# Two groups of transposes in an attention kernel take their PSUM from another ring of buffers

## The chip, the cores and the metric

The kernel runs on one core of a Trainium2 chip. A core has a matrix engine (TensorE, "PE" in the profile, with its weight loads as "PEld"), a vector engine (VectorE, "DVE"), a scalar engine (ScalarE, "ACT"), GpSimd ("POOL") and a queue that issues transfers ("SP"). Each engine works through its own instructions in order and waits on semaphores for the others. TensorE writes its products into PSUM, which VectorE and ScalarE read. The metric is the device time of one execution in microseconds, as a median of several.

## What is computed

The reference is a stack of two transformer layers over four sequences of 1024 tokens with 256 channels. What matters here are its three kinds of attention, all with 16 heads of 16 channels:

```python
x = x + _L0_attn_ref(_layernorm(x), ...)   # causal, with a bias that grows with the key's position
x = x + _L0_ffn_ref(_layernorm(x), ...)    # 4 experts, top 2 of them per token; each expert is an
                                           # attention among the tokens that chose it
x = x + _L1_attn_ref(_layernorm(x), ...)   # causal, with rotary positions
x = x + _L1_ffn_ref(_layernorm(x), ...)    # 64 experts, top 8, and one shared

# each of the first three holds, per sequence and head:
scores = jnp.einsum('bhtd,bhsd->bhts', q, k) * scale
attn = jax.nn.softmax(jnp.where(mask, scores, -inf), axis=-1)
y = jnp.einsum('bhts,bhsd->bhtd', attn, v)
```

## The kernel before, in words

**Units.** An attention is worked off in units: four heads (one of four groups `g`) of up to 512 queries of one sequence. A sequence of 1024 tokens has two halves of queries, so 8 units; an expert's sequence has as many query tiles of 128 as its fullest batch needs, in one or two halves. In the profiled execution there are 160 units: 32 in the attention of layer 0, then 32, 16, 16 and 32 in the four experts (six, two, three and seven tiles, as the widths of the instructions show), then 32 in the attention of layer 1. `nq` is the number of a unit's query tiles (2 to 4).

**Two passes over the scores.** The scores are computed twice. First with queries on the partitions: two heads of a pair against up to 512 keys (L294, tile `s1`), of which VectorE takes the row maxima (L309; in causal attention it first adds a mask to the diagonal block, L306). These are the *products for maxima*. When a unit has all its maxima, `set_max` reduces and negates them (L365), transposes them on TensorE (L372, tile `pm`, one transpose for each query tile), and VectorE adds the result into a spare row of the queries (L376), so that the second pass has the maximum already subtracted. In the second pass keys are on the partitions: L329 writes one bank for each of two heads (tile `s2`), ScalarE takes the exponential out of each (L340), and L394 multiplies by the values, for all keys of the unit into one bank (`av`). These are the *products for exponentials*. In causal attention L353 adds a mask to the diagonal ones.

**The end of a unit.** `divide` lets ScalarE copy the finished `av` into SBUF (L408, tile `avs`), TensorE transposes it (L412, tile `py`), and VectorE takes the reciprocal of the sums (L416) and multiplies (L417).

**Ticks.** The order of TensorE, VectorE and ScalarE is written out by hand in `_run_attention`. In each tick it emits, for TensorE: one step of maxima of a unit that is ahead (the two heads of one L294 pair), one step of exponentials of a unit that is behind (the two heads of an L329 pair), the masks, and the L394 of the step one to three ticks earlier; for VectorE the reduction of this tick; for ScalarE the exponentials. `next_max` picks the two steps so that they use different strips of the matrix engine, and the profile shows their products overlapping. A unit's exponentials come `lead` ticks after its maxima. Then, at the end of the tick, one to a few of the *running parts* get a step, in rotation: `set_max`, `divide`, the projections of queries, keys and values (L177, L194), the output projection (L436, L445), a layer norm's transposes (L104), the transposes of an expert's rows (L939). A part that something needs at once is run to its end (`settle`). So the transposes of `set_max` and `divide` stand at the end of a tick, ahead of the next tick's L294.

**PSUM.** `open_attention` lays out all of it, counted in banks of 512 floats on each partition:

```python
self.ps = ctx.enter_context(tc.tile_pool(name="ps", bufs=2, space=PSUM))
self.ps_m = ctx.enter_context(tc.tile_pool(name="ps_m", bufs=3, space=PSUM))
self.ps_av = ctx.enter_context(tc.tile_pool(name="ps_av", bufs=1, space=PSUM))
```

`ps` is a ring of two buffers of two banks. The products for maxima take one buffer a tick, and so does each of the running parts that project or transpose (tags "s"). `ps_m` is a ring of three buffers of one bank; the products for exponentials take two a tick (tag "t"), and in the kernel before `pm` and `py` take one each. `ps_av` is one bank. A tile of a ring takes the buffer that was taken longest ago, in the order in which the program asks; its first write waits until the last reader of that buffer's earlier tile is done. At the end of a run of the attention, when no maxima are left, a tick does two steps of exponentials, the second in a buffer of `ps` (tile `s3`, L346).

Of the kernel before, what the change touches and what calls it, by code (L numbers as in the profile page):

```python
# [10 lines left out]
F32 = mybir.dt.float32  # L11
# [10 lines left out]
P = 128  # L22
# [22 lines left out]
class Kernel:  # L45
# [313 lines left out]
    def set_max(self, u):  # L359

        nc = self.nc
        nq = u["nq"]
        self.n_mx += 1
        m = self.mx_buf[self.n_mx % 2]
        nc.vector.tensor_reduce(  # L365
            m[:, 0:nq, :, ROW_MAX], u["mx"][:, 0:nq, :, 0 : u["n_half"]], AX.X, ALU.max, negate=True
        )
        yield
        yield
        pm = self.ps_m.tile([P, 512], F32, tag="t", name="pm")  # L370
        for q in range(nq):
            nc.tensor.transpose(  # L372
                pm[:, q * P : (q + 1) * P], m[:, q].rearrange("p h r -> p (h r)"), self.ident
            )
        part = u["qk"][0][:, u["q0"] : u["q0"] + nq * P]
        nc.vector.tensor_tensor(part, pm[:, 0 : nq * P], part, ALU.add)  # L376
        yield
# [25 lines left out]
    def divide(self, u):  # L403

        nc = self.nc
        g, nq, i0 = u["g"], u["nq"], u["q0"] // P
        avs = self.p2.tile([P, 512], F32, tag="avs", name="avs")
        nc.scalar.copy(avs[:, 0 : nq * P], u["av"][:, 0 : nq * P])  # L408
        yield
        pt = self.ps_m.tile([P, 4, 4, 32], F32, tag="t", name="py")  # L410
        for q in range(nq):
            nc.tensor.transpose(  # L412
                pt[:, q].rearrange("p h r -> p (h r)"), avs[:, q * P : (q + 1) * P], self.ident
            )
        rec = self.p2.tile([P, 4, 4], F32, tag="rec", name="rec")
        nc.vector.reciprocal(rec[:, 0:nq], pt[:, 0:nq, :, HD])  # L416
        nc.vector.tensor_tensor(  # L417
            u["job"]["y"][:, i0 : i0 + nq, 64 * g : 64 * (g + 1)].rearrange(
                "p q (h d) -> p q h d", d=HD
            ),  # L420
            pt[:, 0:nq, :, 0:HD],
            rec[:, 0:nq].unsqueeze(3).to_broadcast([P, nq, 4, HD]),
            ALU.mult,
        )
        yield
# [39 lines left out]
    def _run_attention(self, jobs, causal):  # L465
# [76 lines left out]
        for tick in range(len(ahead) + lead + 4):  # L542
# [40 lines left out]
            for u in full:  # L583
                if divides[1:]:
                    settle(divides[-2])
                begin("divide", u, divide(u), True)
                divides.append(u["divide"])
                if u["g"] == NG - 1 and u["last"]:
                    begin("finish", u, finish(u))
                    ended.append(u["finish"])  # L590
# [1022 lines left out]
```

## Time and profile before

| | |
|---|---|
| median of 7 runs | 4624.06 us (4615.11 to 4635.45) |
| the profiled execution | 4632.74 us |
| its span, first to last instruction | 4631.0 us |
| busy: TensorE, VectorE, ScalarE, GpSimd | 4354.3, 2634.8, 1910.5, 628.4 us |
| granted clock of TensorE, mean | 0.954 |

By stretches of the span (us, busy time of each engine, granted clock):

| stretch | what runs | PE | DVE | ACT | clock |
|---|---|---|---|---|---|
| 0 to 950 | attention of layer 0 | 891.06 | 609.77 | 400.29 | 0.95 |
| 950 to 1745 | expert of six tiles | 765.78 | 444.65 | 384.82 | 0.96 |
| 1745 to 1925 | expert of two tiles | 161.06 | 78.21 | 64.41 | 0.98 |
| 1925 to 2200 | expert of three tiles | 252.87 | 133.33 | 109.14 | 0.97 |
| 2200 to 3150 | expert of seven tiles | 928.67 | 574.28 | 486.31 | 0.97 |
| 3150 to 4300 | attention of layer 1 | 1054.29 | 695.54 | 381.45 | 0.92 |
| 4300 to 4631 | the rest of the experts of layer 1 | 300.56 | 99.03 | 84.11 | 0.97 |

How to read what follows. A row of the timeline has a start and a duration in microseconds, then the engine, the line of the kernel, the operation, what it writes and reads, and the shapes; "x2" means two instructions merged into one row. A bracket tells how long the engine was idle before it and whose release ended that. A group's row ends with the busy time of all its instructions, the mean of one in ns, and the idle time before them with the releasers. "issue" is idle time that no release ended. Matmuls are pipelined, and their ends are modelled, so a busy TensorE isn't one at its peak.

The two groups of the change, from the tiles' views: the 544 instructions of L372 have a median of 273 ns (270 to 476), those of L412 too (272 to 477); L376 comes 160 times (414 to 693 ns), L416 160 times (198 to 259 ns), L417 160 times (291 to 426 ns).

### The profile page before, as it was taken

To read this page: it belongs to the slowest core of one execution; us is meant where nothing else is said; L and a number is where in the kernel's file an instruction comes from. 1 tells how busy PE (TensorE), PEld (TensorE's weight loads), DVE (VectorE), ACT (ScalarE), POOL (GpSimd) and SP (SyncE) were. 2 spreads that over 40 slices of the span, in tenths; PEclk is the share of its full clock that TensorE was granted. 3 is DMA by queue.
4 is the path that set the end of the run, shared out by engine and by line. 5 is a ranking of instruction groups with operands and counts; after the bars stand their busy time and mean duration, and the time that the engine had idled before them with its cause. 6 is when DMAs were issued, how large, how long until landed. Compare 5 with 4: busy or idle time off the path is not lost.

```text
span 4631.0 us, 88434 instructions
## 1 busy us (share of the span) xinstructions
PE 4354.3 (94%) x38042; PEld 2055.4 (44%) x38042; DVE 2634.8 (57%) x4505; ACT 1910.5 (41%) x4087; POOL 628.4 (14%) x671
## 2 busy tenths in 40 slices
PE   7999999979999999898999999997999999998898
PEld 3444445444444445444343434443444444443556
DVE  5766676646556544454666666655767566474232
ACT  1444444525555553343454545451343333233331
POOL 1002020110000000000001010102111423415243
PEclk8999999979999999999999999998999899898999
DMA  6004000010000000000000000001000111102576
GB/s 217 2 2 136 6 20 4 29 39 8 8 8 8 8 30 25 23 26 26 1 9 27 14 27 1 27 10 32 6 1 28 65 37 49 58 29 88 139 183 176
DMA packets 134455, 188.93 MB, mean 41 GB/s; under 512 B 14816, under 2 KB 116448, under 8 KB 133216
## 3 DMA queue, kind: packets, MB, share of 16 engines
q1 hardware_dynamic: 91584, 99.11, 6.8%
q0 software_dynamic: 27264, 66.18, 5.1%
q10 hardware_dynamic: 15136, 17.20, 1.2%
q8 instruction: 314, 5.14, 0.5%
q14 instruction: 157, 1.29, 0.1%
HBM read 83.36 MB, written 99.09 MB: 39 GB/s over the span
## 4 chain that ended last, share of the span: by engine, by line
PE 64%; DVE 6%; issue 5%; DMA 2%; ACT 1%; another core or an unknown queue 1%; POOL 0%; SPq 0%; POOLq 0%; DVEq 0%; ACTq 0%
PE s L294 20%; PE av L394 12%; PE s L329 8%; PE pq L177 3%; PE pa L177 3%; PE pb L177 2%; PE pk L177 2%; DVE mx L309 2%; PE pv L194 2%; PE po L445 2%; PE pgu L1292 2%; PE py L412 1%; PE pm L372 1%; DMA xg<-xs 1%; PE s L353 1%
## 5 line engine op out<-in xcount | busy, mean ns | idle before, releaser
L340 ACT ACTIVATE e<-s 128x512 f32<-128x512 f32 (+3 forms) x3428 | 1546.1, 498 | 1857.2 <-PE s L329 1065.7
L309 DVE TENSOR_REDUCE mx<-s 128x2 f32<-128x1024 f32 (+3 forms) x1760 | 1724.8, 981 | 757.1 <-PE s L329 600.5
L329 PE MATMUL s<-qa,ka 32*128 32x384 f32 (+3 forms) x7040 | 1882.2, 557 | 58.6 <-ACT e L340 31.1
L294 PE MATMUL s<-ka,qa 32*128 32x384 f32 (+3 forms) x7040 | 1709.0, 565 | 69.3 <-DVE mx L309 27.2
L394 PE MATMUL av<-e,v 128*32 128x256 f32 (+3 forms) x14080 | 949.7, 346 | 22.2 <-ACT e L346 11.2
L294 PEld LDWEIGHTS s<-ka,qa 32*128 32x128 f32 x7040 | 551.3, 190 | 673.0 <-issue 406.3
L329 PEld LDWEIGHTS s<-qa,ka 32*128 32x128 f32 x7040 | 721.9, 187 | 139.4 <-ACT e L340 68.7
L394 PEld LDWEIGHTS av<-e,v 128*32 128x32 f32 x14080 | 298.7, 111 | 793.6 <-issue 711.8
L306 DVE TENSOR_TENSOR s<-s,mask 128x256 f32<-128x256 f32 x512 | 218.8, 427 | 244.2 <-PE s L294 184.5
L975 POOL DMA_DIRECT2D xc<-os x24 | 18.1, 756 | 2004.3 <-DVE os L971 2004.3
L1270 POOL DMA_INDIRECT xs<-rowsx,dest x192 | 185.4, 966 | 222.9 <-DVE dest L1269 155.4
L353 PEld LDWEIGHTS <-ident_b 128*32 128x32 bf16 x4096 | 62.6, 96 | 244.6 <-issue 231.0
L353 PE MATMUL s<-mask_kq,ident_b 128*32 128x128 bf16 x4096 | 154.3, 231 | 0.0
L177 PE MATMUL pq<-xT,wq 128*128 128x512 f32 (+2 forms) x384 | 149.6, 528 | 2.0 <-ACT xT L942 1.7
L93 POOL TENSOR_SCALAR rows<-x,rstd,shift 128x256 f32<-128x256 f32 x96 | 52.1, 558 | 720.7 <-DVE shift L82 710.9
L445 PE MATMUL po<-wo,yT 128*128 128x256 f32 x544 | 129.7, 390 | 11.5 <-ACT yT L440 11.5
L177 PE MATMUL pk<-xT,wk 128*128 128x512 f32 (+2 forms) x384 | 139.1, 499 | 0.1
L963 DVE SCALAR_TENSOR_TENSOR ka<-pk,bk,kc 128x768 f32<-128x768 f32 (+3 forms) x64 | 52.3, 818 | 152.5 <-PE pk L177 152.5
L1441 POOL DMA_INDIRECT sum<-ye,idx x64 | 100.0, 1562 | 161.0 <-DVE ye L1439 115.1
L376 DVE TENSOR_TENSOR qa<-pm,qa 128x512 f32<-128x512 f32 (+2 forms) x160 | 97.1, 607 | 40.7 <-PE pm L372 37.5
L958 ACT ACTIVATE qa<-pq,bq 128x768 f32<-128x768 f32 (+3 forms) x64 | 47.4, 741 | 173.8 <-PE pq L177 173.8
L445 PEld LDWEIGHTS po<-wo,yT 128*128 128x128 f32 x544 | 101.1, 192 | 36.9 <-ACT yT L440 17.2
(205 smaller groups left out, 3271.3 us busy)
## 6 DMA issues: line engine op xcount, KB each, us to landing
xc<-empty SPq DMA_DIRECT2D x4, 4096.0 KB
gu<-in_e_gu SPq DMA_DIRECT2D x64, 256.0 KB
xs<-empty ACTq DMA_DIRECT2D x16, 642.0 KB
xg<-xs SPq DMA_DIRECT2D x64, 160.5 KB
dn<-in_e_dn SPq DMA_DIRECT2D x64, 128.0 KB
sum<-sum SPq DMA_DIRECT2D x12, 512.0 KB
rows<-xc SPq DMA_DIRECT2D x19, 256.0 KB
xc<-os POOLq DMA_DIRECT2D x8, 512.0 KB
```

Source lines behind the costliest of these rows:

```text
L177: nc.tensor.matmul(pt[:, h, 0:wd], lhsT=w[:, c, g * P : (g + 1) * P], rhs=xnT[:, c, h * 512 : h * 512 + wd], start=(c == 0), stop=(c == 1),)
L294: nc.tensor.matmul(s[:, jj, 0:w], lhsT=qa[r : r + 32, q0 : q0 + P], rhs=ka[r : r + 32, k0 : k0 + w], start=True, stop=True,)
L306: nc.vector.tensor_tensor(d, d, self.mask.unsqueeze(1).to_broadcast([P, 2, P]), ALU.add)
L309: nc.vector.tensor_reduce(mx, s[:, :, 0:w], AX.X, ALU.max)
L329: nc.tensor.matmul(t[:, 0 : end - q0], lhsT=ka[r : r + 32, kt * P : (kt + 1) * P], rhs=qa[r : r + 32, u["q0"] + q0 : u["q0"] + end], start ...
L340: lambda e=e, t=t, jj=jj, w=end - q0: nc.scalar.activation(e[:, jj, 0:w], t[:, 0:w], AF.Exp)
L353: nc.tensor.matmul(t[j : j + 32, 0:P], lhsT=self.ident_b[:, j : j + 32], rhs=self.mask_kq, start=False, stop=True, skip_group_check=True,)
L376: nc.vector.tensor_tensor(part, pm[:, 0 : nq * P], part, ALU.add)
L394: nc.tensor.matmul(u["av"][32 * j : 32 * j + 32, c0:c1], lhsT=v[:, kt, c : c + 32], rhs=e[:, j % 2, c0 - q0 : c1 - q0], start=(first and h ...
L445: nc.tensor.matmul(po[:, q, :], lhsT=yT[:, q, c, :], rhs=wo[:, c, :], start=(c == 0), stop=(c == 1),)
L1270: d = nc.gpsimd.indirect_dma_start(out=self.xs[int(last)][:, :], out_offset=bass.IndirectOffsetOnAxis(ap=at, axis=0), in_=rows[:, i, :], i ...
L1441: nc.gpsimd.indirect_dma_start(out=of[:, :], out_offset=bass.IndirectOffsetOnAxis(ap=idx[:, 0:1], axis=0), in_=ye, in_offset=None, compute ...
```

## The change

`pm` and `py` become the first bank of a buffer of `ps`, the ring of two that the products for maxima use, where they were a bank of `ps_m`, the ring of three that the products for exponentials use. Nothing else is touched; the instructions, their order on each engine and their shapes are the same.

```diff
 def set_max(self, u):
...
-        pm = self.ps_m.tile([P, 512], F32, tag="t", name="pm")
+        pm = self.ps.tile([P, 2, 512], F32, tag="s", name="pm")[:, 0, :]
         for q in range(nq):
             nc.tensor.transpose(
                 pm[:, q * P : (q + 1) * P], m[:, q].rearrange("p h r -> p (h r)"), self.ident
...
 def divide(self, u):
...
-        pt = self.ps_m.tile([P, 4, 4, 32], F32, tag="t", name="py")
+        pt = self.ps.tile([P, 2, 4, 4, 32], F32, tag="s", name="py")[:, 0]
         for q in range(nq):
             nc.tensor.transpose(
                 pt[:, q].rearrange("p h r -> p (h r)"), avs[:, q * P : (q + 1) * P], self.ident
```

## The prediction

> **What bounds the kernel now.** I read the page first, its chain and its groups, then the list of waits, then the two tiles that the change moves, and last the timeline around single places where they are written.
>
> ```profile
> PE 64%; DVE 6%; issue 5%; DMA 2%; ACT 1%; another core or an unknown queue 1%; POOL 0%; SPq 0%; POOLq 0%; DVEq 0%; ACTq 0%
> ...
> L309 DVE TENSOR_REDUCE mx<-s 128x2 f32<-128x1024 f32 (+3 forms) x1760 | 1724.8, 981 | 757.1 <-PE s L329 600.5 <-PE s L294 114.5 <-remote 6.3
> L329 PE MATMUL s<-qa,ka 32*128 32x384 f32 (+3 forms) x7040 | 1882.2, 557 | 58.6 <-ACT e L340 31.1 <-issue 12.8 <-DVE qa L376 10.0
> L294 PE MATMUL s<-ka,qa 32*128 32x384 f32 (+3 forms) x7040 | 1709.0, 565 | 69.3 <-DVE mx L309 27.2 <-DVE ka L963 22.8 <-POOL ka L1062 6.6
> ```
>
> TensorE sets the end: 64% of the chain, VectorE 6%, ScalarE 1%. It works in order, and one tick of the attention on it is the products for maxima (L294), the products for exponentials (L329), then the exponentials times V (L394). The reductions (L309) wait for TensorE far more than it waits for them, so a stall put into TensorE's queue is paid unless VectorE was late at that place anyway. The waits on the two rings of PSUM, in the list (us in total, times, longest):
>
> ```profile
> PEld s L294 <- DVE mx L309: 93.8, 184, 2.6
> PEld s L329 <- ACT e L340: 68.7, 96, 4.8
> ```
>
> The first is the ring of two, where the change adds; the second the ring of three, where it takes away.
>
> **What the change does to the order.** It adds no instruction and removes none: 544 transposes at L372 and 544 at L412 stay where they are in TensorE's queue, at a median of 273 ns, and no transfer is issued, dropped or moved past another. What moves is which release each write waits for. Call the products of a tick S(n), and their reduction R(n). The ring of two gives S(n) one buffer and S(n+1) the other, so S(n+1) waits for R(n-1), long done. A transpose at the end of tick n now takes the buffer of S(n-1) and waits for R(n-1); S(n+1) gets the buffer of S(n) and waits for **R(n), the reduction that has just started**. S(n+2) waits for the eviction of the transposes (L376 or L417). The ring of three is left to the exponentials alone.
>
> **The new wait, at one place of each kind.** The first attention, a unit's maxima with full width (start, duration):
>
> ```profile
> 602.78 1.21 DVE L309 TENSOR_REDUCE mx<-s 128x2 f32<-128x1024 f32 x1
> ...
> 603.10 0.66 PE L372 MATMUL pm<-ident,mx 128*128 128x128 f32 x4
> 603.68 0.70 PE L294 MATMUL s<-ka,qa 32*128 32x512 f32 x2
> 603.70 0.70 PE L329 MATMUL s<-qa,ka 32*128 32x512 f32 x2
> 603.91 0.68 DVE L376 TENSOR_TENSOR qa<-pm,qa 128x512 f32<-128x512 f32 x1
> 604.86 1.23 DVE L309 TENSOR_REDUCE mx<-s 128x2 f32<-128x1024 f32 x1 [0.21 <-PE s L329]
> ```
>
> R(n) ends at 602.78 + 1.21 = 603.99. Where a weight load of L294 waited for L309 in this trace it started 0.054 us after the reduction's end (median of 186 such waits), so S(n+1) would start at 604.05 in place of 603.68: 0.37 us. Behind it stand the four L329 of the tick and eight L394, and behind those the exponentials and R(n+1). S(n+2) waits for L376, done at 604.59, and doesn't start before 605.3: nothing. An expert of six tiles:
>
> ```profile
> 1522.85 0.96 DVE L309 TENSOR_REDUCE mx<-s 128x2 f32<-128x768 f32 x1 [0.38 <-PE s L329]
> ...
> 1523.18 0.55 PE L372 MATMUL pm<-ident,mx 128*128 128x128 f32 x3
> 1523.66 0.59 PE L294 MATMUL s<-ka,qa 32*128 32x384 f32 x2
> ```
>
> Here 1523.81 + 0.05 - 1523.66 = 0.20 us. And the second causal attention, in a stretch in which VectorE is late because it also routes:
>
> ```profile
> 3848.49 0.19 PEld L294 LDWEIGHTS s<-ka,qa 32*128 32x128 f32 x2 [0.20 <-DVE mx L309]
> ...
> 3849.27 1.22 DVE L309 TENSOR_REDUCE mx<-s 128x2 f32<-128x1024 f32 x1
> ...
> 3850.40 0.68 DVE L376 TENSOR_TENSOR qa<-pm,qa 128x512 f32<-128x512 f32 x1
> ...
> 3850.53 0.30 PEld L294 LDWEIGHTS s<-ka,qa 32*128 32x128 f32 x4 [0.53 <-DVE mx L309]
> ...
> 3851.91 1.22 DVE L309 TENSOR_REDUCE mx<-s 128x2 f32<-128x1024 f32 x1
> ```
>
> S(n+1) would move from 3848.49 to 3850.54, 2.05 us later. But it lasts about 1.2 us with its L329, so it ends at 3851.7, before 3851.91, when VectorE has finished L376 and its routing and takes the next reduction. VectorE loses nothing there. TensorE is some 0.7 us behind afterwards (its next two ticks hold 1.2 + 0.5 us each and no longer wait).
>
> **The sum.** I read the same two rows at all 320 places (160 units, L372 and L412): end of the last reduction plus 0.054, less the start of the next write into the ring of two. Late by, in us:
>
> | part of the span | after L372 | after L412 |
> |---|---|---|
> | attention of layer 0 (32 units) | 13.4 | 7.6 |
> | expert of six tiles (32) | 5.5 | 0.7 |
> | experts of two and three tiles (32) | 5.9 | 1.8 |
> | expert of seven tiles (32) | 5.7 | 5.1 |
> | attention of layer 1 (32) | 22.6 | 15.1 |
>
> That is 83.3 us (rounding aside), at 198 places. 172 of them are under 1 us and hold 43.9; these I count in full. Four, with 12.0, lie where both VectorE and ScalarE sat idle for over 3 us on TensorE's own results (at 4209, for one), so that the start shown for L294 can't be trusted: I count nothing, bounds 0 and 12.0. The other 22, with 27.4, are of the third kind above, where 0.7 of 2.05 was left, or in between: half, 13.7, bounds 9 and 27.4. Together 57.6.
>
> The transposes' own new wait, for R(n-1), is late at few places: 5.5 us in all.
>
> Then what is **taken away**. The transposes no longer wait for an exponential (idle time before them, from the tiles' views, L372 then L412):
>
> ```profile
>   ACT e L340: 8.9, 25
> ...
>   ACT e L340: 17.9, 56
> ```
>
> 26.8 us at 81 places, but 0.20 us before a transpose is there without any releaser ("issue"): 26.8 - 81 x 0.20 = 10.6 gained. And in the tick behind the transposes the second L329 comes a bank earlier to its turn: it then waits for the first exponential of tick n, not the second (0.54 us earlier at 512 columns, 0.44 at 384). The four L329 of those ticks take, summed over all places, 26.7 us more than undisturbed ones do (0.81 us at 384 columns, 1.13 at 512, and 0.1 of ordinary spread). Undisturbed ticks have such a delay in every second tick, so part of it only moves one tick on: I take half, 13.3, bounds 0 and 26.7.
>
> Waits for two engines cost L372 78 separate semaphore instructions of 51 ns (4.0 us); with the new ring L372 waits for VectorE alone, and L412 for ScalarE and VectorE, up to 160 x 0.051 = 8.2 us. They run while the array drains: 0, bounds -4.0 and +8.2.
>
> In the last ticks of each run of the attention the ring of two also serves pairs of exponentials; these are in the 320 places, and small.
>
> 57.6 + 5.5 - 10.6 - 13.3 = **+39 us**. The profiled execution took 4632.74 us (span 4631.0), 8.7 above the median; on the median of 4624.06 it gives **4663 us**. All costs at their upper and all gains at their lower bound give 83.3 + 5.5 + 8.2 = +97.
>
> **Two rules beside the rows.** The Trainium skill speaks against this change: its page Perfetto Trace Analysis, Optimizing Tensor Performance (Matmuls), wants independent groups to rotate through different banks, so that one's eviction overlaps the next group's products; here S(n+1) gets the buffer whose eviction is running. Taken at its word each of 320 places would pay a whole eviction, 320 x 0.98 = 314 us; the rows show the transposes and L394 covering all but 83.3 of that. The page TensorE: Matmul & The Clock Gate, "A second HAM failure mode: psum-queue depth-cycling", says that small idle gaps from cycling through PSUM make the clock fall back. The granted clock here is 0.92 in the stretch from 3150 to 4300 us and 1.00 from 1440 to 1720; one hundredth of it over the span would be 46 us, which is not in the sum.
>
> **Rivals.**
>
> 1. *The forecast*, +39, 4663 us: 45%.
> 2. *VectorE's lateness hides nothing and the gains are phase shifts*: each new wait is paid in full, and the lower clock of layer 1 gets lower with the gaps. For it: at 184 places L294 already waits for L309. Against it: the third timeline. +97, 4721 us: 25%.
> 3. *Nothing to be measured*: TensorE's waits change places, and the ring of three gives back what the ring of two takes; also the case that the transposes' buffer comes free as before. For it: gains of up to 10.6 + 26.7 stand against the 43.9 that is certain, and the third timeline's absorption may hold for smaller waits. 4624 us: 15%.
> 4. *The other side: the ring of three is the true limit.* ScalarE's exponentials decide when L329 may start, at the second L329 of every other tick; the transposes out of the way, the whole 10.6 + 26.7 is gained, and the later S(n+1) only fills time in which L329 would have waited. -37, 4587 us: 15%. It decides if the delay of L294 behind a transpose comes out under 37.3 / 320 = 0.12 us a place; the two timelines above show 0.37 and 0.20, which speaks against it.
>
> A difference under 0.2% (9 us) can't be told from none here. Rival 3 is "same", rival 4 nearly all of "faster"; with the forecast's own spread (+39, from 20 to 60) almost nothing is added to either: faster 0.14, same 0.16, slower 0.70. The range goes from the edge of "same" below, 4615, to rival 2's full sum, 4721.
>
> **What would show it.** In the changed profile: L294's waits for L309 grow from 93.8 + 27.2 us by some 60 and come right behind L372 and L412; the waits of L372 and L412 for L340 vanish, and L329's for L340 fall by some 10; L309's busy time stays at 1725; the granted clock stays near 0.954. The forecast is wrong if L294 behind a transpose isn't released by L309 (then the rings work otherwise than read), if those waits appear and the span doesn't grow (absorption, rival 3 or 4), or if the clock falls by more than 0.01 (rival 2).

## The result, and the profile after

The changed kernel takes 4661.33 us (median of 16 runs, 4649.27 to 4671.23) against 4627.01 us of the kernel before (40 runs, 4614.38 to 4643.45): 34 us more, a ratio of 1.0072 with a 95% interval of 1.0063 to 1.0081. Its profiled execution took 4657.57 us, with a span of 4655.9; the granted clock was 0.953, against 0.954.

The page of the changed kernel, its chain (shares of the span by engine, then by engine and line) and the groups that the prediction showed of the kernel before:

```profile
PE 81%; DVE 12%; issue 2%; DMA 2%; ACT 2%; another core or an unknown queue 1%; POOL 1%; ACTq 0%; SPq 0%; DVEq 0%; POOLq 0%
PE s L294 27%; PE av L394 14%; PE s L329 9%; DVE mx L309 7%; PE pq L177 4%; PE pk L177 4%; PE pv L194 3%; PE po L445 3%; PE pa L177 3%; PE pb L177 2%; PE pgu L1292 2%; PE s L353 2%; PE py L412 1%; DVE s L306 1%; PE ph L1422 1%
...
L309 DVE TENSOR_REDUCE mx<-s 128x2 f32<-128x1024 f32 (+3 forms) x1760 | 1725.4, 981 | 772.0 <-PE s L329 617.3
L329 PE MATMUL s<-qa,ka 32*128 32x384 f32 (+3 forms) x7040 | 1874.4, 560 | 39.6 <-ACT e L340 22.7
L294 PE MATMUL s<-ka,qa 32*128 32x384 f32 (+3 forms) x7040 | 1716.2, 567 | 131.1 <-DVE mx L309 67.1
```

The same work is done: L309 is busy for 1725.4 us, where it was 1724.8. TensorE still has most of the chain. What grew is the idle time before L294. The list of waits (us in total, times, longest):

```profile
PEld s L294 <- DVE mx L309: 143.7, 284, 2.7
...
PE s L294 <- DVE mx L309: 67.1, 137, 2.2
PEld s L329 <- ACT e L340: 58.1, 97, 3.9
```

The two lines of L294 add up to 210.8 us where they were 121.0, before 421 instructions where it was 236. Not all of the 90 us are new time. At many places the weight load and the product behind it both stand idle, and the two lines count the same stretch twice. And the idle time before L294's weight loads that no release ended fell from 406.3 to 367.0 us, with 181 fewer of such gaps: some 0.2 us each were idle before as well, under another name. The gaps tell it without counting twice; a *gap* here is time, from TensorE's first instruction on, in which its rows show neither a product nor a weight load. The gaps that end with L294 grew by 59.8 us, from 67.6 to 127.4. Those that end with L329 fell from 57.4 to 39.0. All gaps together grew by 41.6 us, from 240.5 to 282.1, and the busy time of TensorE fell by 18.3, from 4354.3 to 4336.0. So the longer span is gaps before L294, in part made good elsewhere.

One place, the six-tile expert of the prediction, now (start, duration; the bracket is the idle time before and its end):

```profile
1539.01 0.96 DVE L309 TENSOR_REDUCE mx<-s 128x2 f32<-128x768 f32 x1 [0.38 <-PE s L329]
...
1539.34 0.55 PE L372 MATMUL pm<-ident,mx 128*128 128x128 f32 x3
1539.93 0.56 DVE L376 TENSOR_TENSOR qa<-pm,qa 128x384 f32<-128x384 f32 x1
1540.02 0.19 PEld L294 LDWEIGHTS s<-ka,qa 32*128 32x128 f32 x2 [0.37 <-DVE mx L309]
...
1540.03 0.59 PE L329 MATMUL s<-qa,ka 32*128 32x384 f32 x2
```

The reduction ends at 1539.97 and L294 starts at 1540.02, 0.68 us after L372 where it was 0.48: the 0.20 us that the prediction had for this place. The row of L329 beside it takes 0.59 us. Before, the same row took 0.73, because its second product waited for an exponential (L340) that ended at 1523.77:

```profile
1523.67 0.73 PE L329 MATMUL s<-qa,ka 32*128 32x384 f32 x2
```

Both programs have the same order on TensorE, so L294 number k of one can be set against number k of the other. The shift that arises in each part (us), beside the lateness that the prediction's table summed there (L372 and L412 together):

| part | lateness in the table | shift, first pair of profiles | shift, second pair (another chip) |
|---|---|---|---|
| attention of layer 0 | 21.0 | +13.9 | +10.0 |
| expert of six tiles | 6.2 | +3.1 | +3.7 |
| experts of two and three tiles | 7.7 | +4.8 | +6.4 |
| expert of seven tiles | 10.8 | +2.1 | +4.9 |
| attention of layer 1 | 37.7 | +3.9 | +8.2 |

The second pair is from runs e7 and e8 below. The spans differ by 24.9 and 39.5 us; single executions of one kernel scatter by up to 16 us to either side, so a pair of profiles gives the places better than the total.

In the second pair the gaps do the same: those before L294 grow from 64.3 to 125.1 us, those before L329 fall from 48.8 to 40.8, and TensorE's busy time falls by 20.2 us. In both pairs the products of L294 and L329 run side by side for longer: 1560.3 us against 1531.0, and 1552.9 against 1524.7, more than half of the difference in the attention of layer 1.

### The profile page after: what moved, and what is told of

It is laid out like the page before. It is cut to its first block, busy times and chain, and to the rows that moved or that the text cites. A ratio compares the mean times of both kernels' runs of the same rounds, so it can differ in the third digit from the quotient of the medians.

```text
span 4655.9 us, 88426 instructions
## 1 busy us (share of the span) xinstructions
PE 4336.0 (93%) x38042; PEld 2034.5 (44%) x38042; DVE 2635.0 (57%) x4505; ACT 1908.0 (41%) x4087; POOL 626.8 (13%) x671
## 3 DMA queue, kind: packets, MB, share of 16 engines
q14 instruction: 155, 1.27, 0.1%
## 4 chain that ended last, share of the span: by engine, by line
PE 81%; DVE 12%; issue 2%; DMA 2%; ACT 2%; another core or an unknown queue 1%; POOL 1%; ACTq 0%; SPq 0%; DVEq 0%; POOLq 0%
PE s L294 27%; PE av L394 14%; PE s L329 9%; DVE mx L309 7%; PE pq L177 4%; PE pk L177 4%; PE pv L194 3%; PE po L445 3%; PE pa L177 3%; PE pb L177 2%; PE pgu L1292 2%; PE s L353 2%; PE py L412 1%; DVE s L306 1%; PE ph L1422 1%
## 5 line engine op out<-in xcount | busy, mean ns | idle before, releaser
L340 ACT ACTIVATE e<-s 128x512 f32<-128x512 f32 (+3 forms) x3428 | 1545.1, 498 | 1880.9 <-PE s L329 1084.5
L309 DVE TENSOR_REDUCE mx<-s 128x2 f32<-128x1024 f32 (+3 forms) x1760 | 1725.4, 981 | 772.0 <-PE s L329 617.3
L329 PE MATMUL s<-qa,ka 32*128 32x384 f32 (+3 forms) x7040 | 1874.4, 560 | 39.6 <-ACT e L340 22.7
L294 PE MATMUL s<-ka,qa 32*128 32x384 f32 (+3 forms) x7040 | 1716.2, 567 | 131.1 <-DVE mx L309 67.1
L294 PEld LDWEIGHTS s<-ka,qa 32*128 32x128 f32 x7040 | 555.8, 190 | 747.2 <-issue 367.0
L329 PEld LDWEIGHTS s<-qa,ka 32*128 32x128 f32 x7040 | 706.8, 188 | 108.8 <-ACT e L340 58.1
L416 DVE RECIPROCAL rec<-py 128x16 f32<-128x16 f32 (+2 forms) x160 | 38.3, 240 | 138.6 <-PE py L412 131.1
```

The lines of the kernel that those rows point to most:

```text
L294: nc.tensor.matmul(s[:, jj, 0:w], lhsT=qa[r : r + 32, q0 : q0 + P], rhs=ka[r : r + 32, k0 : k0 + w], start=True, stop=True,)
L309: nc.vector.tensor_reduce(mx, s[:, :, 0:w], AX.X, ALU.max)
L329: nc.tensor.matmul(t[:, 0 : end - q0], lhsT=ka[r : r + 32, kt * P : (kt + 1) * P], rhs=qa[r : r + 32, u["q0"] + q0 : u["q0"] + end], start ...
L340: lambda e=e, t=t, jj=jj, w=end - q0: nc.scalar.activation(e[:, jj, 0:w], t[:, 0:w], AF.Exp)
```

## The experiments

Each run was timed against the kernel before on its own chip, in turns. The chips differ: on two of them (the first chip and that of e7 to e10) the kernel before takes 4616 to 4627 us at a granted clock near 0.954, on three others 4470 to 4475 us near 0.971. These are called slower and faster chips below. Most of that lies in the attention of layer 1: from its first L294 to its last e4 below, on a faster chip, takes 983 us, the kernel before on the first chip 1082, at a clock of 0.97 against 0.93. L329's waits for exponentials differ too. The kernel before on the first chip, then e4, all of L329 (us, times):

```profile
  ACT e L340: 99.8, 117
```

```profile
  ACT e L340: 25.5, 85
```

72 of the 99.8 us lie in the attention of layer 1, but 9 of the 25.5. So differences of times are taken on one chip alone, and what a run on a faster chip shows of the ring of three need not hold on the first chip.

| run | what it is | time | before beside it | ratio (95%) |
|---|---|---|---|---|
| e1 | only L372 in the ring of two | 4512.5 | 4474.6 | 1.0083 (1.0069 to 1.0096) |
| e2 | only L412 in the ring of two | 4505.9 | 4474.6 | 1.0064 (1.0051 to 1.0078) |
| e3 | changed, L329 ahead of L294 behind transposes | 4492.8 | 4474.6 | 1.0043 (1.0029 to 1.0057) |
| e4 | before, and a small product in the own bank | 4479.2 | 4469.5 | 1.0025 (1.0015 to 1.0036) |
| e5 | before, and it takes a buffer of the ring of two | 4520.4 | 4469.5 | 1.0117 (1.0102 to 1.0132) |
| e6 | changed, and a small product in the own buffer | 4525.0 | 4469.5 | 1.0125 (1.0110 to 1.0141) |
| e7 | before | 4612.1 | 4615.6 | 0.9994 (0.9982 to 1.0006) |
| e8 | changed | 4655.4 | 4615.6 | 1.0092 (1.0071 to 1.0114) |
| e9 | before, and it takes one more bank of the ring of three | 4677.7 | 4615.6 | 1.0127 (1.0106 to 1.0148) |
| e10 | before, L329 ahead of L294 in every tick | 4596.3 | 4615.6 | 0.9961 (0.9948 to 0.9975) |
| e11 | changed, L329 ahead of L294 in every tick | 4516.6 | 4474.0 | 1.0099 (1.0082 to 1.0117) |
| e12 | e1 once more | 4508.8 | 4474.0 | 1.0077 (1.0062 to 1.0091) |

### The cost without the gain: e4, e5, e6

The change does two things at once: it puts a tile into the ring of two and takes one out of the ring of three. A small product that nothing reads, ahead of the transposes, separates them.

```diff
+    def touch(self, bank):
+        self.nc.tensor.matmul(
+            bank[0:32, 0:P], lhsT=self.ident_b[:, 0:32], rhs=self.mask_kq,
+            start=True, stop=True, skip_group_check=True,
+        )
...
# e4, and e6 on the changed kernel: into the transposes' own tile
+        self.touch(pm)
# e5: into a buffer of the ring of two; pm and py stay in the ring of three
+        self.touch(self.ps.tile([P, 2, 512], F32, tag="s", name="extra")[:, 0, :])
```

e4, the control:

> A control: the kernel before, with one small product (bf16, 128 columns, as those of L353) written into the transposes' own bank just ahead of them, which they overwrite. No ring is touched. 320 such products at 0.04 to 0.1 us: +13 to +32 us on before, by every theory.

e5:

> The same small product, but into a buffer taken from the ring of two; the transposes stay in the ring of three. This is the cost of the change without its gain: the next product for maxima must wait for the reduction just started, while the ring of three stays as it was. Against e4_touch_own, theory A (forecast: loss 57.6 + 5.5, gains 10.6 + 13.3): +50 to +65 us, clearly more than the change's +34. Theory C (the ring of three gives back nothing, its delays only move on; the loss itself is smaller than I summed): the same +34 as the change.

e6:

> The changed kernel with the same small product in the transposes' own buffer. Against e4_touch_own it is the change once more on another ground: +34 us by every theory, if small shifts of phase don't decide. Against e5_touch_ring2 it is what freeing the ring of three gives: -15 to -30 us by theory A, 0 by theory C.

e4 came out at +9.7 us, just under what was expected for 320 small products. e5 is 41.2 us above e4: the wait alone. e6 is 45.8 us above e4: the change. So taking the transposes out of the ring of three, for which the forecast had counted 23.9 us of gain, gave back nothing here: e6 is 4.5 us above e5, not below. The mean granted clock of e6's four runs was 0.9698, that of e5's 0.9715, which is worth up to 0.0018 x 4520 = 8 us, so without it the gain would be 3 us at most. The waits of e4, then of e5:

```profile
PEld s L294 <- DVE mx L309: 89.2, 184, 2.8
```

```profile
PEld s L294 <- DVE mx L309: 137.2, 284, 2.8
...
PE s L294 <- DVE mx L309: 66.0, 144, 2.2
```

These are nearly the 143.7 and 67.1 us of the changed kernel, without any change to the ring of three. Of TensorE's gaps, those before L294 are 65.8 us in e4, 111.4 in e5, 114.5 in e6. Those before L329 are 15.3, 9.0 and 8.9: they fall as much in e5, where the ring of three is as before. So on this chip L329 waits less because L294 ahead of it is held up and ScalarE has that time, not because a bank is free. That is theory C, though e5's 41 us lie a little above its 34. On the slower chips, where L329 has more to wait for, this pair wasn't run: there the change lowers L329's gaps by 18.4 and 8.0 us, and whether a part of that is the freed bank stays open. By the shift of L294, e5 and e6 also keep 19.9 and 16.9 us over e4 in the attention of layer 1, where the slower chips kept 3.9 and 8.2.

### What a bank of the ring of three is worth: e9

```diff
# before, with the small product of e4 in one more bank of the ring of three
+        self.touch(self.ps_m.tile([P, 512], F32, tag="t", name="extra"))
```

> The kernel before with the small product in one more bank of the ring of three, so that this ring's turn is moved by two banks at each place, not by one: the cost that the change takes away, doubled. Against e4_touch_own theory C (the ring of three gives nothing back): within 5 us. Theory A (a bank of this ring is worth 24 us of waits): +15 to +30 us.

+62 us on before, and the control for its product was about 10 (e4, on another chip): both theories missed it. The idle time before the transposes says why. L372, which is line 379 there:

```profile
  ACT e L340: 73.4, 172
```

and L412, line 420 there:

```profile
  ACT e L340: 68.9, 200
```

With one bank taken at the end of a tick, the transposes get the one that was last used a tick earlier: 26.8 us of waits for exponentials in the kernel before, most of it idle time that is there anyway. With two banks taken they get one of this tick's, whose exponential has just begun: 142.3 us, in which a weight load and its product can again count twice. TensorE's gaps before the transposes are 47.8 us, where e7, the kernel before on this chip, has 5.3: about the 50 us that e9 costs beyond its product. The ring has room for one tile at that place and not for two, which fits that taking the one out saved nothing.

### The parts alone: e1, e2, e12

e1 is the first half of the diff, e2 the second.

> Only the transposes of the maxima (L372) take a buffer of the ring of two; those of the values stay in the ring of three. Theory A (the wait of the next product for the reduction just started sets the price, so the price follows the late places of the table: 53.1 us of lateness after L372, most of it counted, less a small gain): +25 to +35 us on before, that is most of the change's +34. Theory B (the price comes from somewhere that both moves share alike, such as a lower clock or the ring itself): half of it, about +17.

> Only the transposes of the values (L412) take a buffer of the ring of two. Theory A: 30.3 us of lateness after L412, of which more than half sits at places where VectorE is late and that count half or nothing, and 17.9 us of waits for exponentials that go away: 0 to +10 us on before. Theory B: about +17. If the two parts don't add up to the change's +34 within some 8 us, they act on one another.

> e1_pm_only once more, because its mean granted clock was 0.966 against 0.971 of the kernel before beside it, worth up to 0.0045 x 4490 = 20 us of its +38. If the clock falls again by 0.004 or more: +30 to +40 us. If it stays within 0.002: +15 to +25 us, and the two parts then add up to about the change's own price without a fall of the clock.

e1 came a little above its range, e2 far above: +37.9 and +31.3 us. They don't add up to the change, which is +34 and +40 on its two chips and +46 on the ground of e4. The clock may be part of it. The mean granted clock of e1's runs was 0.9666 and of e2's 0.9672, with 0.9707 for the kernel before beside them. The difference is worth up to 0.0041 x 4490 = 18 us of e1's and 16 of e2's; without it they are 20 and 16. In e12 the clock was 0.9680 against 0.9706, 12 us of +34.8; a fall of 0.0026 lies between the two cases that its expectation named. So with the whole of the clock set aside the halves are 20 to 23 and 16 us, and their sum, 36 to 39, is close to e5's 41 (clock 0.9715 against 0.9714 of e4).

The gaps don't show such a sum. Those before L294 are 106.6 us in e1, 107.0 in e12 and 86.2 in e2, against 65.8 in e4: 41 and 20 more, where both together, in e5, have 46 more. And TensorE's busy time is no longer in e1 and e12 (4257.3 and 4254.8 us) than in e4 (4263.6, with its small products). So by the gaps L372 alone has nearly the whole wait, and the halves act on one another. How much of e1's and e2's price is the clock's stays open, and so does why it fell. It fell with both halves too, by less: by 0.0015 in e8 and 0.0022 in e6 against the kernel before beside them. Theory A fits in that most is L372's, but L412's part isn't near zero.

### Filling the wait: e3, e10, e11

The order of the two kinds of products within a tick is free. In e3 it is turned round in the ticks right behind transposes of the changed kernel, in e10 and e11 in all ticks.

```diff
 def both(self, a, b, causal, c=None):
...
+        swap, self.swap = self.swap, False      # e10, e11: swap = True
+        if a is not None and not swap:
+            products()                          # the L294 of this tick
         for part in (b, c):
...
+        if a is not None and swap:
+            products()
         for t in masks:
...
# in set_max and in divide, behind the transposes
+        self.swap = True
```

> The changed kernel, but in the tick right after such transposes the products for exponentials (L329) are issued ahead of the products for maxima (L294), so that TensorE has work while the reduction runs out. Theory A: the new wait is 0.2 to 0.4 us at most places, and the L329 last 0.6 to 1.1 us, so most of the wait is filled; what remains is the overlap of the two kinds lost at these places: the time falls from 4661 to 4630 to 4650 us. Theory B (the price isn't this wait): 4661 or more, since the overlap is lost and nothing is won.

> The kernel before with the products for exponentials issued ahead of the products for maxima in every tick. It tells whether the waits for reductions that the kernel before has already (121 us in all on L294) can be filled in the same way as e3_swap fills the new ones: if so 20 to 60 us faster than before. Against it: the second product for exponentials waits for ScalarE at 117 places (100 us), and the products for maxima would then stand behind those waits: 0 to +40 us. I take the second.

> The changed kernel with the products for exponentials ahead of the products for maxima in every tick. In e10_before_swap_all the waits of L294 for reductions fell from 116 to 50 us and L329's waits for exponentials rose from 99 to 249. Theory A: with this order the change's own wait is covered by the L329, and freeing the ring of three takes away some of the L329's waits, so it comes out at e10's -19 us or better, -15 to -35 us on before. Theory C (freeing the ring of three gives nothing): the cover is only partial as in e3_swap, so it comes out between e10 and before, -15 to +10 us. I take C.

e3 is 18.2 us above before, where the change was 34 to 46 above on the other chips (it wasn't run on this one): about half of the price is gone, with the same two rings and the same clock (0.9706 and 0.9707). The gaps before L294 (line 295 there) are 61.6 us, as without the change; those before L329 are 39.5, where e4 has 15.3. The waits of its weight loads for reductions, beside e4's 89.2 and e5's 137.2:

```profile
PEld s L295 <- DVE mx L310: 96.8, 166, 2.6
```

So it is this wait that makes the price, as e5 shows from the other side. That the new order alone saves time can't be ruled out by e3, for e10 below is faster with it; but e11, with the changed rings and this order everywhere, is not.

e10 went against what I took: 19 us faster than before. The waits before L294 (line 295 there) and L329 (line 334), from the two lines' own views:

```profile
  DVE mx L310: 50.2, 62
```

```profile
  ACT e L345: 248.9, 576
```

L294's waits for reductions fall from 115.5 us (e7) to 50.2, as the first theory had it. L329's waits for exponentials rise from 98.7 to 248.9, as the second had it, but they take the place of idle time before the first products of a tick: TensorE's gaps are 232.8 us in all, where e7 has 226.7. The gain isn't in the gaps but in its busy time, 4326.4 us against 4353.2 at nearly the same clock (0.955 in both profiles). It lies in the experts of six and seven tiles (-7.6 and -17.0 us by the shift of L294); the attention of layer 0 loses 11.0. A better overlap of the two kinds isn't what the rows show: they run side by side for 1529.4 us, against 1524.7. What is shorter is the time of L329's own rows, 1855.3 us against 1879.0; why isn't shown. Beside the kernel before on its own chip it is the only version that is faster, on the one chip on which it ran.

e11 fell outside both theories: +42.6 us. Its gaps are smaller than those of any other run, 167.3 us; its busy time is 4307.7 us, where e4 has 4263.6 and e12 4254.8. Here the overlap is what changed: L294 and L329 run side by side for 1418.6 us, where e4 has 1518.9 and e12 1530.7. So the order that shortens TensorE's busy time with the old rings lengthens it with the new ones, by products that no longer overlap. Why they don't is open.

### The kernels on one chip: e7, e8

> The kernel before, profiled beside the experiments on their chip, where it takes some 4470 us and not 4625: same time as before, by every theory. Its profile is to show where the two chips differ (theory: in the attention of layer 1, by a higher granted clock) and is the base for the stage by stage comparison.

> The changed kernel on the same chip. If its parts add up: 38 + 31 = +69 us. If the change is as on the first chip: +34. By the pair e6_after_touch_own against e4_touch_own: +46, which I expect (40 to 50), and with it that each part alone costs more than its share, because the part that stays behind in the ring of three keeps its waits for exponentials.

The chip turned out to be one of the slower sort, so that its profile of before is no base for e1 to e6. The two gave the second pair of shifts above, and the change's price once more: +39.8 us, just under the 40 to 50 that were expected.

## Why the prediction was right, and where it wasn't

**The time.** 4663 was forecast, 4661.3 measured; by the difference, +39 was forecast and +34 measured, and +40 on the other slower chip.

**The order of the rings: right.** L294 behind a transpose is released by L309, in the place where the prediction had it. Of its other signs, L294's waits for L309 grew by 90 us in the list, which counts twice, where some 60 was forecast; by the gaps before L294 it is 60. L340 no longer appears among the releasers of the transposes, and L309's busy time and the clock stayed. L329's waits for exponentials fell from 99.8 to 80.8 us, where some 10 was forecast.

**The lateness, 83.3 us: right, place by place.** From the start of the last transpose to that of the next L294, summed over the places where both follow within 6 us (154 and 143 of the 160), the changed kernel takes 50.4 us more behind L372 and 30.4 more behind L412. The table had 53.1 and 30.3.

**What is absorbed: right in kind, rough in size.** In the stretch where VectorE is late, the place at 3847.88 of the kernel before looks like this now:

```profile
3876.11 0.66 PE L372 MATMUL pm<-ident,mx 128*128 128x128 f32 x4
3876.88 1.22 DVE L309 TENSOR_REDUCE mx<-s 128x2 f32<-128x1024 f32 x1
3878.01 0.68 DVE L376 TENSOR_TENSOR qa<-pm,qa 128x512 f32<-128x512 f32 x1
3878.15 0.70 PE L294 MATMUL s<-ka,qa 32*128 32x512 f32 x2 [1.39 <-DVE mx L309]
...
3879.52 1.22 DVE L309 TENSOR_REDUCE mx<-s 128x2 f32<-128x1024 f32 x1
```

The next two reductions start 2.64 us apart, as before the change (3849.27 and 3851.91). L294 is shifted by 1.56 us and two ticks later by 0.36; the prediction had 2.05, then 0.7. In the attention of layer 1 the table's 37.7 us left 3.9 and 8.2. In the first attention less was absorbed than was allowed for: the place at 603 shifted L294 by 0.29 us (forecast 0.37) and it stayed; one at 315, counted half, kept 1.12 of 1.27. And some small waits, counted in full, were absorbed: the 0.20 us at 1523 are 0.02 ten us on, for the L329 beside it waits less than before. The other way of absorbing wasn't in the sum at all: L294 and L329 overlap by 28 to 29 us more, and TensorE's busy time falls by some 20.

**The gain of 23.9 us from the ring of three: wrong, as far as it was tested.** This is the step that failed: "taken away" held 10.6 us for the transposes' own waits and 13.3 for L329 behind them. e6 against e5 shows on a faster chip that freeing the ring gives nothing (+4.5 us, or a gain of 3 at most with the clock set aside). There L329 waits as much less in e5, where no bank is freed, as in e6, so that this belongs to the absorption of the new stall. **The cost of 63 us (57.6 + 5.5)** was too high by about the same: e5 against e4 has 41. There the two errors cancel, so the closeness of the total is partly luck; the sign and the order of the size are not. On the slower chips, for which the forecast was made, only the total was measured: layer 1 absorbs more there and L329 waits longer for ScalarE, so that how the +34 divides into a cost and a gain stays open.

**The semaphores and the two pages.** The separate semaphore instructions, counted at nothing, were looked for at the wrong lines. L372 has 73 of them now (78 before) and L412 one (3), but L294 has 309 (136) and L329 41 (160). TensorE has 712 in all against 639, at 51 ns each 3.7 us, within the bounds. The Trainium skill's page Perfetto Trace Analysis, Optimizing Tensor Performance (Matmuls), which wants groups to rotate through different banks, was right about the direction here; the 314 us that the prediction worked out from it, a whole eviction at each place, would have been some nine times the measured 34. What the page TensorE: Matmul & The Clock Gate, "A second HAM failure mode: psum-queue depth-cycling", says of a clock that falls back with small idle gaps hardly showed in the change itself (0.954 to 0.953 in the profiles; 0.0015 lower in e8, 0.0022 in e6), and agrees with e1, e2 and e12, where the mean fell by 0.0026 to 0.0041.

**The rivals.** Rival 2, everything paid and the clock lower, is refuted by the absorption in layer 1. Rival 3, nothing to be measured, by the interval. Rival 4, the ring of three as the true limit, by the sign and by its own condition: L294 behind a transpose came 0.27 us later a place (80.8 us at 297 places), not under 0.12. e9 shows that with one more tile in it this ring costs some 50 us.

## What to carry to other kernels

When a tile moves into a ring of two, look at the tile behind it: it gets the buffer that was filled last, and waits for a reader that has just begun. The rows of that reader and of the next writer give the lateness at each place before anything is built, here 83 us forecast and 81 measured; what remains of it in the time depends on which engine was late there, and came to about half. A wait that shows on a ring isn't what the ring costs: part of it is idle time that would be there anyway, and part is counted twice. Taking a tile out of the ring of three gave nothing that could be measured (e6 against e5), and one more tile in it cost some 50 us (e9). Where two things change at once, a small product that nothing reads, put into one ring alone, tells them apart.

## What I had not expected

Chips differ by 3% on this kernel, and most of that lies in one stage, the attention of layer 1. The clock is not the only difference. All six profiles on the two slower chips show ScalarE standing before L340 until something that the profile calls remote (another core or a queue that it doesn't tell); the kernel before on the first chip:

```profile
ACT e L340 <- remote: 52.2, 18, 7.7
```

None of the eight profiles on the three faster chips has such a wait. What it is isn't shown.

The same half of the change cost +37.9 and +34.8 us on two chips, with the clock down by 0.0041 and 0.0026; that is about as much as the whole change costs.

The order of two kinds of independent products within a tick moved TensorE's busy time by 27 us one way (e10 against e7, on one chip), and by some 44 the other way where the rings were changed (e11 against e4, on two chips of one sort, e4 with 320 small products more), with no instruction of them added or removed.
